# Spreading a weight load over 15 DMA engines instead of 14, and loading four fields six pairs apart instead of eight

## The chip, the cores and the metric

The kernel runs on one core of a Trainium2 chip. Its time is device time in microseconds (us). The core computes on four engines that matter here: PE (matrix products), ACT and DVE (elementwise work, both can read the products), POOL (elementwise work in on-chip memory). SP only issues transfers. All transfers of the core, whichever engine issues them, are moved by the same 16 DMA engines. Before the change the kernel takes 749.09 us (median of 3 runs, 747.92 to 752.11).

## The reference

For each of the 496 pairs (i, j) of 32 fields, with i < j, the vectors of field i are multiplied by the pair's own 128 x 128 matrix, and the result is multiplied elementwise by field j. The batch is 1024, everything is float32:

```python
v_i = inputs[:, I_IDX, :]                          # 1024 x 496 x 128
v_j = inputs[:, J_IDX, :]
transformed = jnp.einsum('bpd,ped->bpe', v_i, W)   # W: 496 x 128 x 128
return transformed * v_j                           # 260 MB
```

The host passes the fields as `xt` (field, 128, 1024) and the matrices as `wt` (62 chunks of eight pairs, 128 rows, 8 x 128), and the output comes back with its axes in another order. A row of a chunk in one partition is 8 x 128 x 4 = 4096 bytes.

## The kernel before

The loop of the kernel goes over half pairs: `u` counts them, `q = u // 2` is the pair. The pairs are ordered from field 30 down to field 0, so that field i meets all fields above it. The schedule is written by hand; the order of the statements is the order on each engine.

For each half pair, `first(u)` makes two products on PE (of a high and a low part of field and matrix) and a scaling on ACT, and `second(u)` follows three half pairs later with a third product on PE. When both halves are there, DVE multiplies the 128 x 1024 result by field j and writes it into an output tile (`write`, L246). The first 15 pairs use one exact product instead (L267). ACT, POOL and DVE make the parts of the matrices (`split_w`, L151 to L155) and of the fields (`split_x`, L169 to L171, L337).

**Output tiles.** Pairs are stored in groups: four pairs each up to pair 292 (`FOURS = 73` groups), three pairs each after that. A group of four takes one of the tiles s0, s1, s2 (the twelve slots of `slots`, four each) or g0 to g3; `out_tile` takes the one that was used longest ago. The tiles g0 to g3 are also the homes of fields 1 to 16, four fields each: tile gk is handed out as an output tile only if its group ends by pair `XAT[k] - OWAIT`, and from pair `XAT[k]` on its four fields are loaded into it, `XSTEP` pairs apart (`group_at`, `load_group`, L126). After pair 292 there are only the twelve slots, three to a group, from slot 0 on. A store is issued by ACT (L321) shortly after its group's last pair. DVE can write into a tile only when the tile's last store has landed, and a store has landed when its part on every one of the 16 DMA engines has.

**Weight chunks.** Three buffers hold chunks of eight pairs; `load_w(c)` runs when the oldest one has been split. Most chunks are loaded by SP (L134), 128 rows over 16 engines, eight rows to each. The 25 chunks 12, 14, ..., 60 are loaded apart (`load_apart`): POOL's software queue loads the first `8 * n` rows with the source arranged in `n` runs (L116), so that they go over `n` engines, eight rows to each, and SP loads what is left over all 16 engines (L117). `WAPART` has n = 14 for seventeen of the chunks and n = 12 for eight of them (every third, from the second on). The software queue deals its engines in a round: a transfer over n engines takes the next n of them. `move_on(k)` (L111) is a tiny transfer of 2k rows of 64 bytes over k engines that only turns the round. `move_on(START)` takes engines 0 to 4 (numbers of this round, not of the chip), so the first load begins at engine 5, and three pairs (`BACK`) after each load `move_on(16 - n)` completes the round. So engines 3 and 4 are passed over by every one of the 25 loads, and engines 1 and 2 by those with n = 12.

Of the kernel before, what the change touches and what calls it, by code (L numbers as in the profile page):

```python
# [31 lines left out]

XG = 4
START = 5
WAPART = {c: 12 if k % 3 == 1 else 14 for k, c in enumerate(range(12, 62, 2))}
WLAST = max(WAPART)
BACK = 3
FOURS = 73
NS = 12
XAT = (317, 221, 141, 53)  # L40
OWAIT = 20
XSTEP = 8
SLAG = 2
PB = 4

# [6 lines left out]
def _groups():  # L52

    return [(q, OG) for q in range(0, OG * FOURS, OG)] + [(q, OG - 1) for q in range(OG * FOURS, NQ, OG - 1)]
# [3 lines left out]
def kernel(  # L58
# [22 lines left out]
    nc = tc.nc  # L81
# [12 lines left out]
    def load_x(f, pieces=1, eng=None):  # L94
        if f == 0:

            t = rpool.tile([P, WL, P], F32, tag="w", name="x_0").rearrange("p q e -> p (q e)")
        else:
            t = xpool.tile([P, BT], F32, tag=f"x{f}", name=f"x_{f}")
        s = BT // pieces  # L100
        for k in range(pieces):
            (eng or nc.sync).dma_start(out=t[:, k * s : (k + 1) * s], in_=xt[f, :, k * s : (k + 1) * s])
        x_sb[f] = t

    w_raw = {}
# [3 lines left out]
    def move_on(k):  # L109

        nc.gpsimd.dma_start(out=mark[: 2 * k], in_=xt[0, : 2 * k, :16].rearrange("(b a) n -> a b n", a=k))  # L111

    def load_apart(c):
        n = WAPART[c]
        r = 8 * n
        nc.gpsimd.dma_start(out=w_raw[c][:r], in_=wt[c, :r].rearrange("(b a) m n -> a b m n", a=n))  # L116
        nc.sync.dma_start(out=w_raw[c][r:], in_=wt[c, r:])  # L117

    group = {}

    def load_group(k, m):
        if m == XG - 1:
            group[k] = xpool.tile([P, XG, BT], F32, tag=f"g{k}", name=f"x_g{k}")
        f = XG * k + 1 + m
        x_sb[f] = group[k][:, m, :]
        nc.sync.dma_start(out=x_sb[f], in_=xt[f])  # L126

    def load_w(c, splits=(0, WL), eng=nc.sync):
        w_raw[c] = rpool.tile([P, WL, P], F32, tag="w", name=f"w_{c}")
        if c in WAPART:  # L130
            load_apart(c)
            return
        for a, b in zip(splits, splits[1:]):
            eng.dma_start(out=w_raw[c][:, a:b, :], in_=wt[c, :, a:b, :])  # L134
# [78 lines left out]
    back = {}  # L213
# [3 lines left out]
    ngroup = NF // XG // 2  # L217
    group_at = {q + XSTEP * (XG - 1 - m): (k, m) for k, q in enumerate(XAT) for m in range(XG)}
    assert all(q + 5 < first_q[XG * k + m + 2] for q, (k, m) in group_at.items())
    until = {f"g{k}": q - OWAIT for k, q in enumerate(XAT)}  # L220
    groups = _groups()
# [37 lines left out]
    def first(u):  # L259
        q, h = divmod(u, 2)  # L260
        i, c = pairs[q][0], q // WC
        r = slice(q % WC * P, (q % WC + 1) * P)
        s = slice(h * HB, (h + 1) * HB)
        if h == 0:
            po[q] = po_t[q % PB]
        if q < nq0:
            nc.tensor.matmul(po[q][:, s], w_raw[q // WL][:, q % WL, :], x_sb[i][:, s], start=True, stop=True)  # L267
        else:
            for t in (0, 1):
                m = nc.tensor.matmul(po[q][:, s], w_s[c][t][:, r], x_s[i][t][:, s], start=t == 0, stop=t == 1)  # L270
                apart(m, scaled.get(u - 1) if h else None)
            scaled[u] = nc.scalar.mul(po[q][:, s], po[q][:, s], 1.0 + EPS)  # L272
            apart(scaled[u], taken.get(q - PB), "TensorE's products, which this waits for, have waited for it")

    def second(u):
        q, h = divmod(u, 2)
        i, j = pairs[q]
        r = slice(q % WC * P, (q % WC + 1) * P)
        s = slice(h * HB, (h + 1) * HB)
        if q >= nq0:  # L280
            m = nc.tensor.matmul(  # L281
                po[q][:, s], w_s[q // WC][2][:, r], x_s[i][2][:, s], start=False, stop=True, skip_group_check=True
            )
            apart(m, scaled[u ^ 1])
        g, k = group_of[q]
        if k == 0 and h == 0:
            ots[g] = out_tile(g)
        if q >= NQ - 2:
            write(g, k, s, po[q][:, s], x_sb[j][:, s])
        elif h == 1:  # L290
            taken[q] = write(g, k, slice(0, BT), po.pop(q), x_sb[j])
        ot = ots[g][0]
        n = groups[g][1]
        if q >= NQ - 2:
            stores.append((u + SLAG, rows(g)[:, k, s], ot[:, k, s]))
        elif g in (0, len(groups) - 1):
            if h == 1:
                stores.append((u + SLAG, rows(g)[:, k], ot[:, k]))
        elif k == n - 1 and h == 1:
            stores.append((u + SLAG, rows(g), ot))  # L300

    for u in range(2 * NQ + LAG + SLAG):
        q = u // 2
        if u < 2 * NQ:
            i, j = pairs[q]
            if u % 2 == 0 and j == i + 1 and XG * ngroup < i - 2 - XLEAD:
                load_x(i - 2 - XLEAD)
            first(u)
            if u == 2 * nq0:
                move_on(START)  # L310
            if u % 2 == 0 and q in group_at:
                load_group(*group_at[q])
            if u % 2 == 1 and q in w_at:
                load_w(w_at[q])
            if u % 2 == 0 and q in back:
                c = back.pop(q)
                move_on(16 - WAPART[c] if c < WLAST else 32 - START - WAPART[c])
        if LAG <= u < 2 * NQ + LAG:
            second(u - LAG)
        while stores and stores[0][0] <= u - LAG:  # L320
            nc.scalar.dma_start(*stores.pop(0)[1:])  # L321
        if u % 2 == 1:
            ready = [t for t in todo if t[0] <= q]
            if ready:
                ready[0][2](u)
                todo.remove(ready[0])
        if ring[WB:] and ring[0] in spent:
            ring.pop(0)
            c = ring[WB - 1]
            if c == "x":  # L330
                load_x(0)
            else:
                load_w(c)
            if c in WAPART:
                back[q + BACK] = c
        while later and later[0][0] <= u:
            nc.vector.tensor_tensor(*later.pop(0)[1:], ALU.subtract)  # L337
# [32 lines left out]
```

## Time and profile before

| | us |
|---|---|
| median of 3 runs | 749.09 |
| the execution that was profiled | 747.92 |
| its span, first to last instruction | 746.1 |
| PE busy | 704.6 |
| DVE, ACT, POOL busy | 635.9, 634.2, 595.0 |
| median time to landing, store of three pairs (x67) | 12.9 |
| median time to landing, store of four pairs (x43 from `slots`, x29 from g0 to g3) | 16.6, 14.2 |
| median time to landing, `w` over POOL's queue (14 and 12 engines) | 11.7 |
| median time to landing, `x_g` (fields 1 to 16) | 15.7 |

A "share" of a transfer queue is the time of its packets as a part of 16 engines' span; "to landing" is the time from the issuing instruction to the last of the sixteen completions. "DMA share" in a table of stretches is the mean busy share of the 16 DMA engines in that stretch; it can read 1.01, since a packet's record starts a few ns before the one ahead of it ends.

### The profile page before, as it was taken

Reading aid. Unit: us, or ns where it says so; the run is one execution under the profiler, and the core shown is the slowest. Engines: PE = TensorE matmul, PEld = TensorE weight load, DVE = VectorE, ACT = ScalarE, POOL = GpSimd, SP = SyncE. Lnnn points to the kernel's source line nnn. Section 1 sums busy time; section 2 is a strip of 40 time slices with the busy share of each in tenths; the row PEclk is TensorE's granted clock in tenths of the full one; section 3 lists DMA queues with packets and bytes.
Section 4 is the critical chain, followed back from the end, with each engine's and each line's share of the span. In section 5 each row is a group of like instructions: output and inputs, shape, how many; then the busy total and the mean of one; then the engine's idle time right before and its main releaser. Section 6 shows DMA issues by size and latency. Waiting matters only on the chain.

```text
span 746.1 us, 10344 instructions
## 1 busy us (share of the span) xinstructions
PE 704.6 (94%) x2946; PEld 551.3 (74%) x2946; DVE 635.9 (85%) x550; ACT 634.2 (85%) x1256; POOL 595.0 (80%) x882
## 2 busy tenths in 40 slices
PE   7999999999999999989999949999999999999993
PEld 3577777777878888768778838886787877877782
DVE  4888999999999999969889838997888888988794
ACT  1298999999999999969889947998898999998893
POOL 1789999999999999868878855988797878897660
PEclk9999999999999999989999988999999999999997
DMA  9999999999999999999999997999999999999997
GB/s 346 425 425 428 428 428 428 426 425 425 425 420 425 423 423 426 421 424 425 424 427 424 424 409 297 406 421 422 421 426 421 421 423 423 425 415 422 426 427 321
DMA packets 37096, 310.02 MB, mean 415 GB/s; under 512 B 5680, under 2 KB 5808, under 8 KB 19248
## 3 DMA queue, kind: packets, MB, share of 16 engines
q10 hardware_dynamic: 21888, 261.11, 83.0%
q1 hardware_dynamic: 10720, 37.30, 12.4%
q0 software_dynamic: 4432, 10.96, 3.8%
q8 instruction: 24, 0.39, 0.2%
q14 instruction: 32, 0.26, 0.1%
HBM read 49.29 MB, written 260.05 MB: 415 GB/s over the span
## 4 chain that ended last, share of the span: by engine, by line
PE 64%; DMA 20%; DVE 7%; POOL 3%; issue 2%; ACT 2%; ACTq 0%; DVEq 0%; POOLq 0%
PE po L270 41%; PE po L281 20%; DMA out_dram<-slots 17%; DVE slots L246 5%; PE po L267 4%; DMA out_dram<-ot 3%; DVE xd L337 2%; ACT po L272 2%; POOL wd L155 1%; DVE ot L246 1%; POOL wl L153 1%; POOL xl L170 1%; DMA x<-in_xt_dram 1%; POOL xl L171 0%; POOL wd L154 0%
## 5 line engine op out<-in xcount | busy, mean ns | idle before, releaser
L272 ACT ACTIVATE po<-po 128x512 f32<-128x512 f32 x962 | 553.6, 584 | 80.2 <-PE po L270 63.7
L270 PE MATMUL po<-xh,wh 128*128 128x512 f32 x962 | 383.2, 398 | 22.5 <-DVE slots L246 16.9
L281 PE MATMUL po<-xd,wd 128*128 128x512 f32 x962 | 377.2, 392 | 4.8 <-DVE xd L337 2.4
L270 PE MATMUL po<-xl,wl 128*128 128x512 f32 x962 | 378.2, 393 | 1.4 <-POOL wl L153 1.0
L246 DVE TENSOR_TENSOR slots<-po,x 128x1024 f32<-128x1024 f32 (+1 forms) x257 | 306.5, 1212 | 59.2 <-DMA out_dram<-slots 21.5
L153 POOL TENSOR_TENSOR wl<-w,wh 128x256 fp32r<-128x256 f32 x241 | 185.9, 771 | 71.9 <-ACT wh L151 66.2
L270 PEld LDWEIGHTS po<-xh,wh 128*128 128x128 f32 x962 | 181.8, 189 | 79.8 <-DVE slots L246 33.5
L281 PEld LDWEIGHTS po<-xd,wd 128*128 128x128 f32 x962 | 181.6, 189 | 45.0 <-DVE slots L246 3.2
L270 PEld LDWEIGHTS po<-xl,wl 128*128 128x128 f32 x962 | 181.8, 189 | 41.0 <-POOL wl L153 4.0
L155 POOL TENSOR_TENSOR wd<-wl,wd 128x256 fp32r<-128x256 f32 x241 | 180.7, 750 | 20.1
L246 DVE TENSOR_TENSOR slots<-po,x_g 128x1024 f32<-128x1024 f32 x125 | 150.4, 1222 | 23.0 <-DMA out_dram<-slots 12.0
L246 DVE TENSOR_TENSOR ot<-po,x 128x1024 f32<-128x1024 f32 x105 | 126.6, 1220 | 18.1 <-DMA out_dram<-ot 5.7
L154 POOL TENSOR_SCALAR wd<-wh 128x256 fp32r<-128x256 f32 x241 | 102.1, 424 | 20.5
L151 ACT ACTIVATE wh<-w 128x256 fp32r<-128x256 f32 x241 | 98.6, 410 | 5.7 <-DVE slots L246 3.7
L337 DVE TENSOR_TENSOR xd<-xh,xl 128x512 fp32r<-128x512 f32 x52 | 47.5, 913 | 0.0
L170 POOL TENSOR_TENSOR xl<-x_g,xh 128x512 fp32r<-128x512 f32 x32 | 41.6, 1299 | 0.3
L170 POOL TENSOR_TENSOR xl<-x,xh 128x512 fp32r<-128x512 f32 x20 | 25.8, 1291 | 15.8 <-ACT xh L169 15.5
L171 POOL TENSOR_SCALAR xl<-xl 128x512 fp32r<-128x512 f32 x52 | 34.5, 663 | 4.6
L267 PE MATMUL po<-x,w 128*128 128x512 f32 x60 | 28.3, 629 | 4.0 <-DMA x<-in_xt_dram 4.0
L267 PEld LDWEIGHTS po<-x,w 128*128 128x128 f32 x60 | 11.6, 198 | 19.9 <-issue 13.6
L169 ACT ACTIVATE xh<-x 128x512 fp32r<-128x512 f32 x20 | 12.3, 624 | 11.5 <-DMA x<-in_xt_dram 11.3
L169 ACT ACTIVATE xh<-x_g 128x512 fp32r<-128x512 f32 x32 | 20.0, 625 | 0.0
(8 smaller groups left out, 47.2 us busy)
## 6 DMA issues: line engine op xcount, KB each, us to landing
out_dram<-slots ACTq DMA_DIRECT2D x67, 1536.0 KB, 12.9
out_dram<-slots ACTq DMA_DIRECT2D x43, 2048.0 KB, 16.6
out_dram<-ot ACTq DMA_DIRECT2D x29, 2048.0 KB, 14.2
w<-in_wt_dram SPq DMA_DIRECT2D x36, 512.0 KB, 10.8
x_g<-in_xt_dram SPq DMA_DIRECT2D x16, 512.0 KB, 15.7
w<-in_wt_dram POOLq DMA_DIRECT2D x17, 448.0 KB, 11.7
x<-in_xt_dram SPq DMA_DIRECT2D x14, 512.0 KB, 9.4
w<-in_wt_dram POOLq DMA_DIRECT2D x8, 384.0 KB, 11.7
```

Of the source, the lines that this page charges most:

```text
L151: halved[c] = nc.scalar.mul(h, raw, 1.0 - 2.0**-13)
L153: nc.gpsimd.tensor_tensor(l, raw, h.bitcast(F32), ALU.subtract)
L154: nc.gpsimd.tensor_scalar(d, h.bitcast(F32), EPS, 1.0, ALU.mult, ALU.mult)
L155: nc.gpsimd.tensor_tensor(d, l.bitcast(F32), d.bitcast(F32), ALU.subtract)
L170: nc.gpsimd.tensor_tensor(l, x_sb[f][:, s], h.bitcast(F32), ALU.subtract)
L171: nc.gpsimd.tensor_scalar(l, l.bitcast(F32), 1.0 / EPS, 1.0, ALU.mult, ALU.mult)
L246: i = nc.vector.tensor_tensor(ot[:, k, s], p, f, ALU.mult)
L267: nc.tensor.matmul(po[q][:, s], w_raw[q // WL][:, q % WL, :], x_sb[i][:, s], start=True, stop=True)
L270: m = nc.tensor.matmul(po[q][:, s], w_s[c][t][:, r], x_s[i][t][:, s], start=t == 0, stop=t == 1)
L272: scaled[u] = nc.scalar.mul(po[q][:, s], po[q][:, s], 1.0 + EPS)
L281: m = nc.tensor.matmul(po[q][:, s], w_s[q // WC][2][:, r], x_s[i][2][:, s], start=False, stop=True, skip_group_check=True)
L337: nc.vector.tensor_tensor(*later.pop(0)[1:], ALU.subtract)
```

## The change

Three constants change, and the loads with n = 14 become loads with n = 15: POOL's queue loads 120 rows over 15 engines, and no part of these chunks is loaded by SP any more. The last eight rows are loaded by the software queue too (`rest`), as eight rows over eight engines, three pairs later. Since 15 + 8 + 9 = 32 is two rounds, `go_round` issues the eight rows and a `move_on(9)`, the eight rows first for every second chunk and last for the others, so that the next load begins at engine 5 again. The loads with n = 12 stay as they are.

`XAT` and `XSTEP` change when fields 1 to 16 are loaded, and with `XAT - OWAIT` until when g0 to g3 serve as output tiles.

```diff
-WAPART = {c: 12 if k % 3 == 1 else 14 for k, c in enumerate(range(12, 62, 2))}
+WAPART = {c: 12 if k % 3 == 1 else 15 for k, c in enumerate(range(12, 62, 2))}
-XAT = (317, 221, 141, 53)
+XAT = (313, 219, 141, 52)
-XSTEP = 8
+XSTEP = 6
@@ load_apart
-        nc.sync.dma_start(out=w_raw[c][r:], in_=wt[c, r:])
+        if n == 12:
+            nc.sync.dma_start(out=w_raw[c][r:], in_=wt[c, r:])
+
+    def go_round(c):
+
+        def rest():
+            a, b = [t[120:].rearrange("a (b m) n -> a b m n", b=2) for t in (w_raw[c], wt[c])]
+            nc.gpsimd.dma_start(out=a, in_=b)
+
+        if WAPART[c] == 12:
+            move_on(4)
+        elif c == WLAST:
+            rest()
+            move_on(4)
+        elif c % 4:
+            rest()
+            move_on(9)
+        else:
+            move_on(9)
+            rest()
@@ the loop
-                c = back.pop(q)
-                move_on(16 - WAPART[c] if c < WLAST else 32 - START - WAPART[c])
+                go_round(back.pop(q))
```

## The prediction

> **What bounds the kernel now.** I read the page's DMA rows first, then stages, then the largest wait.
>
> ```profile
> DMA  9999999999999999999999997999999999999997
> ...
> q10 hardware_dynamic: 21888, 261.11, 83.0%
> q1 hardware_dynamic: 10720, 37.30, 12.4%
> q0 software_dynamic: 4432, 10.96, 3.8%
> ```
>
> The 16 DMA engines are busy in every slice but the last and number 25. The queues are the stores (q10), SP's loads (q1) and POOL's software queue (q0). Their shares give the price of a 4096-byte row: q1 is 0.124 x 16 x 746.1 = 1480 us for 37.30 MB, or 0.163 us a row. The trace's packet records have 0.159 us as the median, which I use.
>
> The table of stretches (length, busy time of PE, PEld, DVE, ACT, POOL with counts, granted clock, DMA share, GB/s):
>
> ```profile
> 200.00:300.00 100.00, 99.74 (x435) 80.87 (x434) 92.79 (x81) 94.40 (x189) 92.11 (x137) 1.00 1.01 424
> ...
> 429.00:447.00 18.00, 8.28 (x36) 6.19 (x34) 5.72 (x6) 8.63 (x18) 10.42 (x17) 0.84 0.99 419
> 447.00:466.00 19.00, 18.18 (x72) 14.92 (x73) 16.36 (x15) 14.47 (x29) 10.09 (x17) 0.88 0.74 293
> ...
> 600.00:727.00 127.00, 124.32 (x535) 99.06 (x535) 108.80 (x94) 114.78 (x228) 98.02 (x152) 1.00 1.01 423
> ```
>
> Around 200 to 300 us PE and DMA are both full; later DMA is full and PE has gaps. DMA runs dry once, at 447 to 466 (share 0.74 where 1.01 is usual: 0.27 x 19 = 5.1 us), after PE stood still before it. The waits of 420 to 475 us (total, times, longest) and the chain of waits there (start, length) say why:
>
> ```profile
> DVE slots L246 <- DMA out_dram<-slots: 12.4, 3, 11.4
> ...
> PE po L270 <- DVE slots L246: 10.5, 1, 10.5
> ```
>
> ```profile
> 429.57 16.88 DMA out_dram<-slots
> 446.54 1.24 DVE slots L246
> ```
>
> Pair 292's group writes slots 0 to 2 and must wait for the store issued at 429.57. A store adds one to its semaphore for each DMA engine. These sixteen times are in the trace: median 442.7 us, last 446.5. So **the latest DMA engine sets the wait**, 3.8 us behind the middle one. At the end likewise: the last store's sixteen lie at 742.0 (median) and up to 745.1.
>
> **Which engine is late** no row says, but the packet records allow it: a packet starts 3 to 4 ns before the one ahead of it on its engine ends, so the records can be followed into 16 chains (I did so from 0 to 480 us and from 512 to 720 us). Two chains carry none of the 25 loads' rows: engines 3 and 4. One of them has stores 27 ns slow per 611 ns packet from 40 us on, without rest; the other has bursts from the first load at 125 us on, 40 to 60 ns a packet on average. Two more chains, without rows in the n = 12 loads only (engines 1 and 2), have bursts of about half that. Nearly all other packets take their usual time. At 431 us engines 3 and 4 stand 0 to 1.7 us ahead of the median, at 721 us 0 to 1 us ahead. So **engines 3 and 4 both need about the relief that they have**: 233 - 33 = 200 rows x 0.159 = 31.8 us, which their slowness uses up.
>
> **The change part by part.** *Rows per engine.* A load with n = 14 gives eight rows to 14 engines and, from SP, one row to each of 16; with n = 12 it is eight and two. Now a load with n = 15 gives eight rows to all but engine 4. The extra eight rows go to engines 4 to 11 where they come first (8 loads and the last), and to 13, 14, 15, 0 to 4 where they come last (8 loads). Counted over the 25 loads:
>
> - engine 3: 33 rows before, 17 x 8 + 8 + 16 = 160 now: +127 rows = **+20.2 us**
> - engine 4: 33 and 33. Engines 1 and 2: 169 and 160. Engines 5 to 11: 233 and 225; 12: 216 now; 13 to 15 and 0: 224 now. That is -1.3 to -2.7 us each.
>
> *When it comes.* The software loads start at 125.4 us and end at 682.1:
>
> ```profile
> L116 POOL DMA_DIRECT2D w<-in_wt_dram x25: 622/625/635, 125.4 to 682.1; - x25
> ...
> DMA to landing us min/median/max: 7.3/11.7/14.1
> ```
>
> Fourteen of them are issued by 420.6 us. For engine 3 these make 87 rows in place of 19: +68 rows = +10.8 us; the median engine loses 4.5 rows, -0.7 us. The other eleven make +59 rows = +9.4 us, the median engine -0.6 us.
>
> *The output tiles.* With `XAT[1]` 219, tile g1 may be used up to pair 199 instead of 201, which costs it one group (pairs 196 to 199) and shifts the turn of all later ones. The last three groups of four went to s2, s0, s1; now to s0, s1, s2. So pair 292 waits for the store before the one it waited for: the one issued at 423.98, whose sixteen landings have median 436.9, last 441.6. On even engines that is 4.9 us earlier, and would fill most of the 5.1 us dip. With engine 3 late it doesn't: there this store lands at 436.9 - 0.7 - 1.0 (its lead) + 10.8 = 446.0, against 446.5 before. Then the next two groups wait for engine 3's stores too, 5.5 us apart. So I take -0.5 us up to here.
>
> *After the dip.* Before, all engines ran dry there, and at 479 us all stood within 1.0 us of each other. Engine 3 will not run dry: it comes out of it 9.1 - 5.1 = about 4 us late. To that the second half adds 9.4, and the end comes when its last store lands: 742.0 - 0.6 + 4 + 9.4 + d, where d is its own drift before (0, from the chains), or 754.8 in place of 745.1: **+9.7 us**. With d from -2.2 to +3.1, the spread of the sixteen landings between 680 and 740 us, it is +7.5 to +12.8.
>
> *The rest.* SP issues 17 loads fewer (0.33 us each, it waits most of the time). POOL issues 17 more, 0.63 us each = 10.7 us. POOL is 92% busy at 100 to 300 us, and PE waits 5.0 us for it in all; if all of some six issues there fell on PE it would be 3.8 us, but DMA has 12 to 21 us of stores queued there, which hides it: 0 (0 to 3.8). The eight rows are issued some 4 pairs = 5 us after the load and land within its 14.1 us: 19 us, while the chunk's first split comes 18 pairs x 1.36 = 24 us after the load: 0. If they were late, ACT's `wh` would wait, and POOL and PE behind it, 1 us for each us. The marks grow from 4 to 18 rows of 64 bytes: packets of 13 ns, 17 x 7 x 0.013 = 1.5 us over all engines together: 0.1 us. The x loads come 0 to 10 pairs earlier; their bytes and count are the same. The tightest field has 16 pairs = 22 us until its split (14 before), against 15.7 us to landing. Loaded closer together, four of them bring DMA at most one load (512 KB at 424 GB/s = 1.2 us) ahead of itself: 0, at most 1.2.
>
> *Sum.* 747.92 (the profiled run: span 746.1 and 1.8 around it) - 0.5 + 9.7 = 757.1. That run lies 1.2 below the median of 749.09; so **758** is predicted, with 7.5 to 12.8 and the 0 to 3.8 of POOL as bounds: 753 to 763.
>
> The trace shows no transfer like the new eight rows, whose two sides have the same plain shape. Its nearest rows are the marks: 82 packets of 128 bytes, which is 16 x 2 + 8 x 4 + 5 + 13, so a transfer over k engines does use k and turn the round by k. The Trainium skill ("DMA: Bandwidth & Descriptors", section "Why a DMA increments its semaphore by 16 and not by 1") gives the same rule, but names an exception: some direct copies of the software queue run as k = 16 with the partitions dealt out from engine 0 on. By the rule the sum stands; by the exception the round would not turn by eight, which is rival (A) below. No run here shows it.
>
> **The rivals.** *(A) The round goes astray*: the eight rows turn it by 0, not by 8. Then every load with n = 15 shifts it by 24, half a round; the n = 12 loads pass engines 9 to 12, and the others pass 4 and 12 in turn. Engine 3 has 216 rows (+183 = 29.1 us, 16.4 of it by the dip) and engine 4 has 144. For: the plain shape. Against: the marks. The time: 758 + (29.1 - 20.2) = 767.
>
> *(B) Faster: engine 3's bursts come from being passed over.* They begin with the first load and end with the last, so a load causes them. If an engine that is passed (it gets tiny packets and the mark in place of rows) pays for that, engine 3's slowness goes with its relief; at the dip it stands no later than others once some 9 us of its 17.8 us are gone. Then other engines gain 1.4 us, and the turn of the tiles takes 2 to 4.9 us out of the dip: 749.1 - 1.4 - 3.2 = 744.5. For: engines 1 and 2, passed over less often, have half the bursts. Against: those two show about 0.6 us of it in loads that pass them and 0.4 in loads that don't, where the engine that is always passed shows 1.1; and engine 3 may be the one that is slow without any load.
>
> *(C) Half of it*: engine 3 improves by 5 us in each half and the tiles' turn helps: 749 to 752, 750.5.
>
> **How the numbers follow.** Forecast 0.52, (A) 0.15, (B) 0.17, (C) 0.16. From no change a measurement of this kernel can tell about 0.5%, 3.7 us. Faster by more than that is (B): 0.17. Within it is most of (C): 0.13. Slower: 0.70. The range leaves out about half of (A) and of (B): 745 to 767; the forecast's own is 753 to 763.
>
> **What would show it.** Right: the latest of a store's sixteen landings moves away from the median, to 8 us and more by 430 us and at the end; time to landing of the stores of three pairs rises from 12.9 us by several us; DMA share falls under 1 in the second half, since 15 engines wait for one; DVE's wait for stores grows from 40 us. Engine 3's chain carries 160 rows. Wrong: landings as close as before, the DMA share at 1.01 and no dip at 447 would speak for (B); two engines late, for (A).

## The result, and the profile after

The changed kernel takes 750.19 us (median of 20 runs) where the kernel before takes 747.0 in the same comparison. The ratio, estimated from all these runs, is 1.0037 (95% interval 1.0028 to 1.0047), or +2.8 us. The prediction of 758 us was 8 us too high. In a second comparison (`after_again`) the ratio was 1.0032 (1.0013 to 1.0051).

The profiled execution has a span of 748.0 us (746.1 before). From its page, the DMA row (busy tenths in 40 slices) and the queues (packets, MB, share of 16 engines):

```profile
DMA  9999999999999999999999998999999999999997
...
q10 hardware_dynamic: 21888, 261.11, 82.8%
q1 hardware_dynamic: 10176, 36.18, 12.2%
q0 software_dynamic: 4976, 12.09, 4.3%
```

The dip in slice 25 is there still, but shallower (8 for 7), and 1.1 MB went from SP's queue to the software queue. The table of stretches (same columns as before the change):

```profile
100.00:429.00 329.00, 318.55 (x1363) 252.87 (x1362) 292.80 (x254) 299.57 (x595) 291.54 (x431) 1.00 1.01 423
...
200.00:300.00 100.00, 98.25 (x425) 78.72 (x424) 91.20 (x79) 93.36 (x187) 92.30 (x136) 1.00 1.01 423
429.00:447.00 18.00, 12.48 (x53) 9.43 (x51) 10.52 (x10) 12.39 (x25) 14.48 (x22) 0.91 1.01 422
447.00:466.00 19.00, 18.73 (x76) 15.40 (x77) 16.64 (x15) 15.28 (x30) 11.54 (x19) 0.91 0.84 327
466.00:600.00 134.00, 129.69 (x560) 103.67 (x559) 115.65 (x101) 121.11 (x242) 111.87 (x170) 1.00 1.01 421
600.00:727.00 127.00, 125.03 (x537) 99.29 (x536) 109.59 (x95) 115.11 (x228) 100.48 (x156) 1.00 1.01 420
```

Two of these stretches before the change:

```profile
100.00:429.00 329.00, 321.34 (x1376) 257.74 (x1375) 295.69 (x257) 301.02 (x599) 288.83 (x426) 0.99 1.01 424
466.00:600.00 134.00, 131.89 (x568) 105.05 (x567) 118.00 (x103) 122.96 (x244) 112.11 (x168) 1.00 1.01 419
```

The counts of products (the first count in brackets) tell where time went. From 100 to 429 us PE does 1363 of them (1376 before): 13 late, at 6 products per 1.36 us pair that is 2.9 us. From 429 to 466 it does 129 (108 before): 21 gained. From 466 to 600 it does 560 (568 before): 8 lost again. What the shallower dip gives back had been lost ahead of it, and some is lost again behind it. These are two single executions: up to 100 us, where nothing of the change acts yet, they differ by 5 products too (330, 335 before). The waits of the whole execution (total, times, longest):

```profile
DVE slots L265 <- DMA out_dram<-slots: 31.3, 37, 6.6
PE po L289 <- DVE slots L265: 18.0, 21, 5.7
```

The same waits before the change:

```profile
DVE slots L246 <- DMA out_dram<-slots: 33.5, 35, 11.4
PE po L270 <- DVE slots L246: 16.9, 13, 10.5
```

The chain of waits (start, length) at the dip:

```profile
427.98 17.93 DMA out_dram<-slots
445.99 1.24 DVE slots L265
```

The store that pair 292 waits for is the one before, as foreseen, and DVE's longest wait falls from 11.4 to 6.6 us. What PE waits for DVE in all does not fall, since it now waits more often (18.0 us in 21 waits, 16.9 in 13 before). The store's sixteen landings have a median of 438.0 and a last of 445.9: the latest engine is 7.9 us behind the middle one, 3.8 before. At the end the last store's latest is 4.4 behind, 3.1 before. One engine is late, then, as the forecast had it, and at the dip by about the 8 us that it named. But at the end it is late by far less, and (below) it is not engine 3. The other signs named for the forecast are missing: stores of three pairs land after 12.8 us (12.9 before), the DMA share stays at 1.01 from 600 to 727 us, and DVE's waits for stores come to 33.8 us (40.0 before).

As a measure of lateness I use "latest minus median" of a store's sixteen landings, averaged over the 47 or 48 stores that land from 150 to 430 us, and over those from 480 to 740 us: 3.3 and 2.3 us before, 4.6 and 4.3 after.

**Which engine.** The packet records, followed into 16 chains, give the rows that each engine carried. For loads 5 to 10 of the changed kernel (counted from 0; start in us; one column for each chain; m is a mark packet; loads 7 and 10 have n = 12):

```
5 239.8   9m   9m    8   9m    8   8m   9m    9   9m    8    9    9   8m    8   0m   8m
6 262.8    9    9   8m   1m   8m    8    9   9m    9   8m   9m   9m    8   8m   8m    8
7 285.8    8    8    8    8   0m    8    8    8    8   0m    8    8    8   0m   0m    8
8 305.8   9m   9m    8   9m   8m   8m   9m    9   9m    8    9    9    8    8   0m   8m
9 329.8    9    9   8m   1m    8    8    9   9m    9   8m   9m   9m   8m   8m   8m    8
10 354.2    8    8    8    8    8    8    8    8    8   0m    8    8   0m   0m   0m    8
```

In every load over 15 engines the same eight chains have one row more than the load itself gives them: the last eight rows go to the same eight engines, one each, wherever the round stands. So they don't turn it, and each such load shifts the round by 24, half a turn. Chain 3 (fourth column) is engine 4, the one with 20 to 25 ns more per 611 ns packet all the time. Only loads 0, 3, 6, 9, ... pass over it (its 1 is one of the last eight rows). Engine 12, chain 14, is passed over by the other two thirds. Through the landings, chain 3 is 4.9 us behind the median at 310 us, 6.6 at 415, 2.7 at 481, 4.8 at 584 and 734: engine 4 is the late one. Engine 3 carries all its rows, has no bursts and is not late.

### The profile page after: what moved, and what is told of

Its sections match the earlier page's. It is cut to its first block, busy times and chain, and to the rows that moved or that the text cites. A ratio compares the mean times of both kernels' runs of the same rounds, so it can differ in the third digit from the quotient of the medians.

```text
span 748.0 us, 10339 instructions
## 1 busy us (share of the span) xinstructions
PE 705.9 (94%) x2946; PEld 549.0 (73%) x2946; DVE 635.2 (85%) x550; ACT 635.2 (85%) x1256; POOL 604.9 (81%) x899
## 4 chain that ended last, share of the span: by engine, by line
PE 54%; DMA 28%; DVE 9%; POOL 5%; issue 2%; ACT 0%; ACTq 0%; DVEq 0%; POOLq 0%
PE po L289 34%; DMA out_dram<-slots 23%; PE po L300 17%; DVE slots L265 6%; DMA out_dram<-ot 4%; PE po L286 4%; DVE xd L355 2%; DVE ot L265 1%; POOL wl L172 1%; POOL wd L174 1%; POOL xl L189 1%; POOL wd L173 1%; DMA x<-in_xt_dram 1%; POOL xl L190 0%; ACT po L291 0%
## 5 line engine op out<-in xcount | busy, mean ns | idle before, releaser
L265 DVE TENSOR_TENSOR slots<-po,x 128x1024 f32<-128x1024 f32 (+1 forms) x263 | 313.8, 1213 | 58.5 <-DMA out_dram<-slots 18.8
L265 DVE TENSOR_TENSOR slots<-po,x_g 128x1024 f32<-128x1024 f32 x123 | 147.7, 1222 | 27.7 <-DMA out_dram<-slots 12.5
L265 DVE TENSOR_TENSOR ot<-po,x 128x1024 f32<-128x1024 f32 x99 | 119.7, 1221 | 14.5 <-PE po L300 5.3
L188 ACT ACTIVATE xh<-x 128x512 fp32r<-128x512 f32 x20 | 12.3, 624 | 11.6 <-DMA x<-in_xt_dram 11.4
## 6 DMA issues: line engine op xcount, KB each, us to landing
out_dram<-slots ACTq DMA_DIRECT2D x67, 1536.0 KB, 12.8
```

The lines of the kernel that those rows point to most:

```text
L265: i = nc.vector.tensor_tensor(ot[:, k, s], p, f, ALU.mult)
```

## The experiments

All ratios are to the kernel before, in the same comparison on the same chip. The theories: F, the forecast's, engine 3 has bursts of its own and needs its relief; P, an engine's bursts come and go with its being passed over; R, the eight rows don't turn the round, so engine 4 loses its relief.

| run | ratio (95%) | what it is |
|---|---|---|
| x_only, _again, _third | 1.0006 (0.9978-1.0035), 0.9969 (0.9940-0.9997), 0.9995 (0.9971-1.0019) | new XAT, XSTEP alone |
| fifteen_only | 1.0062 (1.0044-1.0079) | loads over 15 alone |
| after_again | 1.0032 (1.0013-1.0051) | the changed kernel |
| start6 | 1.0002 (0.9985-1.0020) | before, round from engine 6 |
| no_soft | 1.0115 (1.0097-1.0132) | no software loads |
| rows_for_marks | 1.0217 (1.0197-1.0237) | rows in place of marks |
| round_mended | 1.1451 (1.1423-1.1478) | round closed, one mark tile |
| round_two_marks | 0.9969 (0.9947-0.9990) | round closed, two mark tiles |
| all15_two_marks, _again | 0.9971 (0.9957-0.9985), 0.9985 (0.9969-1.0002) | same, no loads over 12 |
| all15_old_x | 1.0012 (0.9993-1.0031) | same, old XAT, XSTEP |
| all15_sp_rest, _again | 0.9927 (0.9902-0.9952), 0.9925 (0.9902-0.9949) | same, last rows by SP |
| all15_sp_rest_more_issues | 0.9995 (0.9976-1.0014) | same, 25 more issues on POOL |
| all15_one_mark | 1.0083 (1.0065-1.0102) | one mark of 34 rows |

**Does engine 3 have bursts of its own?** `start6` moves the round by one engine:

```diff
-START = 5
+START = 6
```

> The kernel before with its round begun at engine 6 in place of 5: the loads with n = 14 pass over engines 4 and 5, those with n = 12 engines 2 to 5. Engine 3 gets 169 rows in place of 33 (+136 x 0.159 = +21.6 us), engine 5 33 in place of 233. Theory F: engine 3's bursts stay with it and it is late by 21.6 us less the 5 us that the dip gives back and its lead: +9 to +16 us, ratio 1.012 to 1.02. Theory P: engine 5 takes over the bursts, engine 3 has half of them: no change, ratio 0.998 to 1.003.

1.0002: no change, where theory F wanted 1.012 at least. What the store packets took beyond their usual 460 and 611 ns, from 150 to 320 us, in us for the eight chains with the most (in brackets the rows of software loads that it carried):

```
before          10.2(0) 7.0(0) 3.1(40) 3.0(40) 2.7(64) 1.0(64) 0.9(64) 0.4(64) ...
start6           9.7(0) 7.1(0) 2.9(40) 2.7(48) 1.9(64) 0.9(56) 0.8(64) 0.6(64) ...
no_soft          4.4(0) 1.5(0) 0.7(0)  0.6(0)  0.4(0)  0.4(0)  0.4(0)  0.4(0)  ...
rows_for_marks   9.4(64) 6.7(64) 4.3(64) 2.6(64) 2.4(64) 1.4(64) 1.1(64) 1.0(64) ...
all15_two_marks  7.0(18) 2.4(66) 2.3(52) 1.3(59) 1.3(63) 1.2(62) 1.2(62) 0.9(65) ...
```

The 7 us are engine 4's even slowness in every line (in `no_soft` the record-following splits it over two chains, 4.4 and 1.5). The 10 us of bursts went from engine 3 to engine 5 with the round, and engine 3 now has the 2.7 to 2.9 of one that is passed over in a third of the loads. Shown: the bursts go with a place in the round that is passed over, not with an engine. Being passed over is not enough for them, though. Engine 4 is passed over by the same loads and shows little beyond its even slowness: 7.0 and 7.1 us here, 5.9 in `no_soft`, where nothing is passed over. Why it is spared is open.

**Is engine 4 alone slow, and does the software queue make the bursts?**

```diff
-WAPART = {c: 12 if k % 3 == 1 else 14 for ...}
+WAPART = {}
```

(the first mark, `move_on(START)`, goes too)

> The kernel before without software loads: all chunks are loaded by SP over 16 engines, eight rows each, and there are no marks. Engine 4 gets 200 rows of the 25 chunks in place of 33, +167 x 0.159 = +26.6 us, less up to 5 us that the dip gives back. Both theories: ratio 1.02 to 1.035. Theory P: only one engine is late, and in 150 to 320 us all others have as little excess of their store packets over the usual 460 and 611 ns as the never passed ones had before (0 to 1 us). Theory F: two engines are late, one of them with 8 us of bursts or more.

Between 150 and 320 us the bursts are gone, in all chains: what the store packets took beyond their usual times is 9.2 us, summed over all engines, where it was 30.2 before. Only one engine is late (8.5 us on the average of 150 to 430 us). Later, packets are slow here too: from 480 to 700 us the same sum is 40.1 us, 48.5 before. So what the run shows of the bursts holds for its first half, and the slow packets of the second half have another cause as well, which was not looked for. The time was overestimated: 1.0115. POOL is spared all its transfers, which matters (below), and the stretch of the dip shows the other reason:

```profile
447.00:466.00 19.00, 11.44 (x43) 9.32 (x44) 10.80 (x10) 8.17 (x16) 4.24 (x8) 0.73 0.49 198
```

DMA share 0.49 in place of 1.01: 0.52 x 19 = 9.9 us without traffic, in which most engines stand idle while the late one catches up. The last landing of a store is 10.6 us behind the median at 414 us, 1.1 us at 483 us, and 3.8 us on the average from 480 us on. Here the dip costs about what the late engine is behind, and then the engines stand even.

**What in the passing makes the bursts?** The marks become rows; nobody is relieved:

```diff
-        nc.sync.dma_start(out=w_raw[c][r:], in_=wt[c, r:])
+    def fill(c):
+        r = 8 * WAPART[c]
+        nc.gpsimd.dma_start(out=w_raw[c][r:], in_=wt[c, r:].rearrange("(b a) m n -> a b m n", a=16 - WAPART[c]))
...
-                move_on(16 - WAPART[c] if c < WLAST else 32 - START - WAPART[c])
+                fill(c)
```

> The kernel before, with the mark of each load replaced by that load's own last rows: eight rows for each of the passed engines (3 and 4, or 1 to 4), three pairs after the load, over the software queue, and nothing by SP. Each engine gets 200 rows of the 25 chunks, so nobody is relieved, as without software loads; but each load still passes over the same engines for its own time. Both: engine 4 late, ratio 1.02 to 1.035. It tells apart what makes the bursts. Theory M (being passed over by a transfer under way slows an engine's store packets): engine 3 has some 10 us of excess in 150 to 320 us as before. Theory A (an engine that has got ahead by its relief is slowed): no relief, no bursts, 0 to 1.5 us of excess.

(In this run the last rows of these chunks lie in another order than the products need; the bytes moved are the same.) Theory A falls: engine 3 has its 64 rows like all others, is 5 to 9 us *behind* the median at 240 to 310 us, and has 9.4 us of bursts all the same. Two engines are late and the time is 1.0217, 0.010 above `no_soft` with the same rows; how much of that is POOL's transfers, which `no_soft` hasn't, these two don't tell. So the price comes with being passed over while a load over 14 (or 12) engines runs, whether or not the rows follow; what in the chip takes it was not found. Per load it is 1.2 to 1.3 us (9.4 to 10.2 us over eight loads), and the relief is 8 rows x 0.159 = 1.27 us: passing over a sound engine gained nothing here.

**Does the round go astray, and what is it worth?** The round is closed by 17 more engines, as if the eight rows didn't turn it (after the last load, `move_on(12)` in place of 4):

```diff
         elif c % 4:
             rest()
             move_on(9)
+            move_on(8)
         else:
             move_on(9)
+            move_on(8)
             rest()
```

> The changed kernel, with the round completed as if the eight rows did not turn it (15 + 17 in place of 15 + 8 + 9). If they do turn it (against R), the loads' starts drift and engine 4 gets most rows: slower than the changed kernel. If they don't (R), every load begins at engine 5 and engine 4 is passed over by all, as it was meant; then theory F (engine 3 has bursts of its own) expects engine 3 late by 20 us of rows: 757 to 759, ratio 1.012 to 1.014 to the kernel before; theory P (bursts follow the passing; engine 4 alone needs relief) expects engine 3 without bursts and no engine late: ratio 0.992 to 0.997, with latest landings within 2 us of the others at 430 us and at the end.

1.1451, which neither theory had. The waits (total, times, longest) name the cause, which lies in the edit: the second mark writes into the tile of the first, so POOL stands until that has landed, 16 times 7.7 us, and PE behind it.

```profile
POOL mark L111 <- DMA mark<-in_xt_dram: 123.9, 16, 12.3
PEld po L291 <- POOL wl L174: 110.8, 16, 10.4
```

With a second tile (`marks[m]` in place of `mark`, and `move_on(8, 1)`):

> The mended round again (15 + 17), with the second mark written into a tile of its own, so that POOL doesn't wait for the first mark to land (123.9 us in the run before). Theory R with P: every load begins at engine 5, engine 4 alone is passed over by all, engine 3 loses its bursts: no engine late, ratio to the kernel before 0.993 to 0.999, and below the changed kernel's 1.0037. Theory F (engine 3 needs its relief for itself): ratio 1.010 to 1.014. If the eight rows do turn the round: above the changed kernel.

0.9969: R and P hold, F falls. Engine 3 has 152 rows or more (160 in the forecast), and the kernel is faster than the changed one and the one before. The latest landing is 1.8 us behind the median from 150 to 430 us, 4.6 in the changed kernel. From 480 to 740 us it is 4.0, hardly less than the 4.3 there, so "no engine late" holds ahead of the dip only. The chains show one and the same engine, the evenly slow one, passed over by every load.

All loads over 15 engines:

```diff
-WAPART = {c: 12 if k % 3 == 1 else 15 for k, c in enumerate(range(12, 62, 2))}
+WAPART = {c: 15 for c in range(12, 62, 2)}
```

> As the mended round, with all 25 loads over 15 engines (none over 12). Theory P: engines 1 to 3 lose the bursts that the eight loads over 12 gave them, and have the rows of the others; engine 4 has a row less in each of eight loads. Nothing is late: 0.993 to 0.999, within 0.002 of the mended round with its loads over 12. Theory F: engines 1 to 3 are late by 9 us and more: 1.010 or above.

> All 25 loads over 15 engines, mended round, last eight rows over the software queue, again beside the two runs below on one chip: 0.9955 to 0.9985, if chips don't matter.

0.9971 and, the second time, 0.9985: no difference from 0.9969 can be claimed.

**The two halves of the change.** `fifteen_only` keeps `XAT` and `XSTEP` as they were:

> The changed kernel with the old constants of the field loads: the loads over 15 engines alone. Theory F, the forecast's: engine 3 is late by 20 us of rows, as it has bursts of its own: +9 to +10 us, ratio 1.012 to 1.014. Theory P with R (an engine's bursts come and go with its being passed over, and the eight rows don't turn the round, so engine 4, slow without rest, is relieved by a third of the loads only): engine 4 is the late one, and the tiles' turn doesn't help: the changed kernel's +2.8 us and the 2 to 5 us that the turn is worth, +5 to +8 us, ratio 1.006 to 1.010.

1.0062, as P with R has it, in the lower part. That engine 4 makes it slow isn't shown by this run: its latest landings are 3.6 and 2.8 us behind the median, 3.3 and 2.3 before. And its profiled execution is 13 products behind at 100 us (322, 335 before), where nothing of the change acts yet. Its stretch of the dip:

```profile
447.00:466.00 19.00, 13.49 (x51) 10.99 (x52) 12.59 (x11) 9.91 (x20) 7.09 (x12) 0.75 0.64 244
```

0.37 x 19 = 7.0 us dry, 5.1 before, 3.2 in the changed kernel. And the constants alone:

```diff
-XAT = (317, 221, 141, 53)
+XAT = (313, 219, 141, 52)
-XSTEP = 8
+XSTEP = 6
```

> The kernel before with the two constants of the field loads alone (XAT, XSTEP). The tiles' turn shifts by one group, so pair 292 waits for the store issued one earlier. Theory T (the turn of the tiles is worth what even engines allow): engine 3 and 4 keep their relief, so the store lands about 5 us earlier for pair 292, the longest wait of DVE for slots falls from 11.4 us to about 6.5 (6.6 in the changed kernel), the DMA share at 447 to 466 us rises from 0.74 to 0.84 or more, and the time falls by 2 to 5 us (ratio 0.993 to 0.997). Rival N: the dip is made up for anyway or comes back later: ratio 0.999 to 1.001.

> The constants of the field loads alone, again, since the interval (0.9978 to 1.0035) left open whether the turn of the tiles is worth anything by itself. Theory T: 0.994 to 0.998. Theory N: 0.999 to 1.001 or more.

> The constants of the field loads alone, a third time: 1.0006 and 0.9969 were measured. Theory T (worth about 2 us even with the old round): 0.995 to 0.998. Theory N: 0.999 to 1.002.

1.0006, 0.9969, 0.9995, a mean of 0.9990: -0.7 us, and only one of the three intervals leaves out 1, barely. Yet DVE's longest wait for slots falls to 6.4 to 6.6 us, as theory T had it, and the dip is gone (share 0.95 in two runs), in the third run wholly:

```profile
447.00:466.00 19.00, 19.00 (x85) 15.71 (x84) 16.69 (x14) 17.62 (x36) 14.27 (x22) 1.00 1.00 395
700.00:727.00 27.00, 24.06 (x105) 19.29 (x104) 21.11 (x18) 21.80 (x45) 16.02 (x26) 1.00 0.92 386
```

The share is 1.00 at the dip and 0.92 at 700 us, where nothing was missing before. From 480 to 740 us the latest engine is behind by 4.0, 3.5 and 5.7 us in the three runs, 2.3 before: without the dip nothing sets the engines even, and the gain is given back at the end. That fits `no_soft`; it is a reading of both, not shown by a run that sets only this. In the other two runs the share at 700 us is 0.99, so the 0.92 is of one execution. Where engine 3 and its bursts are out of the way, the same constants are worth more:

> All 25 loads over 15 engines with the mended round, and the old constants of the field loads. If the gain of that kernel (0.9971) is the missing lateness alone: 0.996 to 0.998. If the turn of the tiles has a part of it, as between the changed kernel (1.0037) and the one with the loads alone (1.0062): 0.9985 to 1.002, with DVE's longest wait for slots back above 9 us and the DMA share at 447 to 466 us below 0.9.

1.0012 against 0.9971 and 0.9985: 0.0027 to 0.0041, or 2 to 3 us (three comparisons; the smaller difference is about as large as its uncertainty), with DVE's longest wait at 11.1 and the share at the dip at 0.80, as written.

> The changed kernel again, on the chip of this comparison: ratio 1.002 to 1.006. Outside that, comparisons between chips would not hold to 0.2%, and engine 4 would be slow to another degree here.

1.0032: the two comparisons of the changed kernel agree.

**What POOL's issues cost.** `all15_sp_rest` gives the last eight rows back to SP:

```diff
-        if n == 12:
-            nc.sync.dma_start(out=w_raw[c][r:], in_=wt[c, r:])
+        nc.sync.dma_start(out=w_raw[c][r:], in_=wt[c, r:])
...
-            rest()
             move_on(9)
             move_on(8, 1)
```

> All 25 loads over 15 engines with the mended round, with the last eight rows loaded by SP again, which leaves POOL 25 issues of 0.63 us less (15.8 us). In the run with all loads over 15 engines PE was busy for 191.6 us of 100 to 300 us, 197.9 in the kernel before, and waited for POOL's wl. If POOL's issues cost time: PE back to 194 us or more in that stretch, and a ratio of 0.990 to 0.996. If the DMA engines hide them, as the forecast took it: PE back, but 0.996 to 0.998 as without it.

> As that, with the last eight rows loaded by SP, again: 0.990 to 0.995, that is 0.003 to 0.005 below the run above.

0.9927 and 0.9925: the fastest kernel of this study, -5.5 us. Adding the issues alone, with `move_on(16, 2)` after each round:

> As that, with 25 more software transfers, each a mark of 64-byte rows over all 16 engines into a tile of its own, which turns the round by nothing and gives POOL the 25 issues of some 0.63 us again, with the rows left to SP. Theory I (POOL's issues are the cost, 0 in the forecast): as with the rows on the software queue, 0.995 to 0.999. Theory Q (it is the rows' place: which queue and when): as without these issues, 0.990 to 0.995.

0.9995: theory I, a little above its range of 0.995 to 0.999. Stretches and waits of `all15_sp_rest_again`:

```profile
100.00:200.00 100.00, 96.57 (x413) 76.27 (x412) 91.32 (x80) 91.17 (x182) 92.46 (x134) 1.00 1.01 423
200.00:300.00 100.00, 98.58 (x427) 79.13 (x426) 91.96 (x79) 93.04 (x186) 92.38 (x137) 1.00 1.01 422
```

```profile
PEld po L278 <- POOL wl L161: 7.6, 11, 2.0
PE po L278 <- POOL wl L161: 3.3, 5, 1.6
```

and with 25 more issues:

```profile
100.00:200.00 100.00, 95.39 (x406) 74.85 (x405) 90.49 (x78) 90.02 (x179) 92.45 (x135) 1.00 1.01 419
200.00:300.00 100.00, 96.93 (x418) 77.33 (x417) 90.65 (x78) 91.06 (x182) 92.75 (x139) 1.00 1.01 415
```

```profile
PEld po L279 <- POOL wl L162: 13.8, 18, 2.0
PE po L279 <- POOL wl L162: 6.6, 12, 1.6
```

POOL is as busy in both (92%): it is full here, so an issue of 0.58 us pushes real work back. PE waits twice as often for `wl`, does 840 - 824 = 16 products less (3.6 us), and 423 and 422 GB/s become 419 and 415. The stores queued on the DMA engines don't hide it. Not all of the difference need be POOL's time: with the 25 transfers the store packets from 480 to 700 us also took 50.2 us beyond their usual times, 29.2 without them, summed over 16 engines (1.3 us an engine). In `all15_two_marks_again`, on the same chip, the 25 issues load real rows. That sum is 26.7 us there, PE does 820 products from 100 to 300 us, and the ratio is 0.0060 above that of `all15_sp_rest_again`.

In the kernel before and in the changed one, with 17 issues more, the same wait of PE is

```profile
PE po L270 <- POOL wl L153: 1.0, 2, 0.8
PE po L289 <- POOL wl L172: 2.3, 4, 0.7
```

One mark in place of two would spare 24 issues:

```diff
-            move_on(9)
-            move_on(8, 1)
+            move_on(17)
```

> All 25 loads over 15 engines, the last eight rows by SP, and one mark of 34 rows of 64 bytes over 17 runs in place of two marks over 9 and 8 engines: 24 software transfers less. By the Trainium skill ("DMA: Bandwidth & Descriptors", section "Why a DMA increments its semaphore by 16 and not by 1") 17 has no divisor up to 16 but 1, so this mark would go over one engine and turn the round by one; no run here has shown that yet. If the round closes so, theory I (POOL's issues cost time: 24 or 25 of them 0.006 to 0.007 of the time in the two runs before) expects 0.985 to 0.991, with PE busy above 195.2 us in 100 to 300 us; theory Q expects 0.990 to 0.995. If the round doesn't close, engine 4 is relieved in few loads: 1.003 to 1.015.

1.0083, a time that was named for a round that doesn't close. But the round did close (the chains show the evenly slow engine passed over by every load), and the mark did go over one engine, 24 packets of 2176 bytes, as the rule quoted there has it. PE, however, did only 415 + 430 products in 100 to 300 us, 5 more than with two marks, and later the engines move 405 to 418 GB/s from 550 to 700 us, where they moved 423 to 425. Each of the fifteen other engines gets a packet of 136 bytes for each such mark, and an issue takes 936 ns on average, not 611. The store packets are slower too: from 480 to 700 us they took 73.7 us beyond their usual times, summed over all engines, 29.2 with two marks (2.8 us an engine). What makes them so was not tried. So it is open whether still fewer issues would help.

## Why the prediction was wrong

- *The latest DMA engine sets the wait.* Right. In the changed kernel too, pair 292's wait ends with the last of the sixteen landings (445.9 us). With engine 4 unrelieved (`no_soft`) the time rises by 0.0115, though POOL is spared its transfers there.
- *"Engines 3 and 4 both need about the relief that they have."* This is the step that failed, for engine 3. Its bursts were the effect of its being passed over: they move with the round (`start6`), stay when the relief is taken away and the passing is not (`rows_for_marks`), and are gone from 150 to 320 us when nothing is passed over (`no_soft`). So the +127 rows, which go with the end of these bursts, make engine 3 no later than the others, and the term of +9.7 us built on them was not there: with every round closed, about the same rows on engine 3 give 0.9969 (`round_two_marks`). The evidence was in the prediction, with rival (B): bursts from the first load to the last, half as many on engines passed over less often. It was set aside as one engine might be slow by itself; one engine was, but it was the other one.
- *"A transfer over k engines does use k and turn the round by k."* This is the second step that failed. It is true for the marks (`move_on`), from which it was read, and false for the eight rows, whose two sides have the same plain shape. They go one each to eight fixed engines. The Trainium skill's exception ("DMA: Bandwidth & Descriptors", section "Why a DMA increments its semaphore by 16 and not by 1": some direct copies of the software queue run as k = 16, the partitions dealt out from engine 0 on) agrees with this trace: eight partitions of 4096 bytes, one row on each of the same eight engines in 17 loads. Its price is 1.0037 - 0.9969 = 0.0068, some 5 us, though the run without it has 16 more issues on POOL.
- *The turn of the tiles.* The mechanism is as foreseen: pair 292 waits for the store before, whose last landing came at 445.9 where 446.0 was worked out. That the two meet is luck, as 446.0 came from engine 3's rows and 438.0 + 7.9 from engine 4's lateness. Its size, taken as -0.5 us, is -0.7 by itself (no change within the noise), and -2 to -3 us on top of the loads over 15 engines.
- *POOL's issues, 0 of 0 to 3.8 us.* Mis-sized. 25 more transfers cost 0.0070, 5 us; for the 17 of this change that makes about 3.6, an estimate by proportion, near the upper bound. It may be too high, since that kernel had 24 more marks on POOL already; what PE waits for `wl` grows by only 1.3 us from the kernel before to the changed one. So 1.3 to 3.6 us is as far as the runs tell it. The cover named ("DMA has 12 to 21 us of stores queued there") was none in 100 to 300 us for the 25: POOL is full there, and the engines move 415 to 419 GB/s in place of 422 to 423.
- *The eight rows come in time.* Right: they land 8.5 us after their issue (median; 12.6 at most), and the waits show none for them.

The rivals: (A)'s mechanism acted, but its 767 rested on engine 3 as well; (B)'s acted too. Its 744.5 is a gain of 4.6 us from 749.1, where the closed round gives 0.0031, or 2.3 us; that this makes 744.7 from the 747.0 of the comparison is luck. (C) names nearly the measured time, 750.5, by luck too: the bursts did end, but not by half, and the lost round made up the rest. The two real ones, one of each sign, came together with POOL's issues.

## What to carry to other kernels

When an engine is slow only where it is treated differently, ask first whether the treatment makes it slow: move the treatment by one engine and look again, in every stage and not only in the first. A round kept by hand is to be counted in the packets of each kind of transfer that enters it, since transfers of another shape may not turn it. And an issue on a full engine is work: price it at its duration in the stage where that engine is full, whatever the bottleneck of the whole is. (Here 8 of the 25 issues fall in 100 to 300 us: 4.6 us, and PE lost 3.6 there.)

## What the runs showed that was not expected

- Engine 3, and in `start6` engine 5, passed over by software loads over 14 of 16 engines, loses about as much in slow store packets (1.2 to 1.3 us a load from 150 to 320 us) as the missing rows save (1.27 us). In two loads of `start6` most of it sits in two store packets one behind the other: 16384 bytes in 1049 and 1208 ns in place of 611, at 184 to 186 us, and in 1132 and 1208 ns at 206 to 209 us. Engine 4, passed over by the same loads, doesn't lose it.
- One engine takes 20 to 25 ns more per 611 ns packet from 40 us on, in every kernel whose records were followed, on two chips, with software loads and without.
- In `no_soft`, a stretch in which the DMA engines run dry sets them even again; taking such a stretch away alone gave 0.7 us, with the latest engine 3.5 to 5.7 us behind afterwards in place of 2.3.
